# Softmax row sums kept in SBUF two steps at a time, and a re-ordered end of the last image, in a fused attention and involution kernel

## The chip, the cores and the metric

The kernel runs on one core of a Trainium2 chip. A core has a matrix engine (PE, with a separate row PEld for its weight loads), a vector engine (DVE), a scalar engine (ACT), GpSimd (POOL) and a queue engine (SP) that issues most DMAs. Each engine works through its own list of instructions in order; engines wait for one another through semaphores. The on-chip memories are SBUF, and PSUM [...] to which PE writes its results. The metric is the time of one execution on the device in microseconds, as a median of several runs.

## The reference

The input `x` has 4 images of 512 channels and 64x64 pixels, all in float32. Two layers follow each other. The first is self-attention over the 4096 pixels of an image with 128 inner channels, the second an involution (a 7x7 filter whose weights are computed for each pixel and each of 8 groups of 16 channels) between two 1x1 convolutions:

```python
q = jnp.einsum('oc,bcn->bon', wq, xf) + bq[:, None]      # k and v alike
energy = jnp.einsum('bci,bcj->bij', q, k)
attn = jax.nn.softmax(energy, axis=-1)
out = jnp.einsum('bcj,bij->bci', v, attn)
x = jnp.einsum('oc,bcn->bon', wo, out) + bo[:, None] + x

o1 = relu(affine(conv1x1(x, W1), s1, b1))
w = conv1x1(relu(affine(conv1x1(o1, Wr), sr, br)), Ws) + bs      # 49 taps x 8 groups
o2 = sum over the 49 taps of w[tap] * o1 shifted by the tap
return affine(conv1x1(o2, W3), s3, b3) + x
```

## The kernel before

`fast_path` computes the attention without subtracting the row maximum. At its end it checks that every reciprocal of a row sum lies within `SAFE`; the verdict decides at run time whether `general_path`, a slower form, is run after it. With the inputs here it isn't run.

**Stages.** For each image b, `keys_values` (L396) computes keys and values from the 8 chunks of 512 pixels. `attention` (L544) then goes through the chunks of queries. A chunk has 32 steps of 128 keys: PE computes scores into a PSUM tile `pss`, ACT takes their exponential into an SBUF tile `pt` (L562), PE adds `vT`·`pt` to `po` (L586), and DVE adds `pt` to the running sum `pacc` in a PSUM bank (L591 to L596). Scores run two steps ahead. `pt` has five buffers. In the last image the last two chunks are each split into two halves of 256 queries (L548).

**Finishing a chunk.** `finish_block` (L448) is a generator that is advanced between steps of the next chunk. ACT copies `po` to `on`; DVE sums `sums` over 32x32 blocks (L465); PE spreads the row sums with the matmul `pl` (L471); DVE takes the reciprocal, spreads it by a transpose and multiplies `on` (L480). Four matmuls `pwo` and four DVE operations (L487) give the attention output in `xt`, four matmuls `p1` the 1x1 convolution, and transposes `pp` the pixel-major form, which a DMA stores in `pix`. The pauses between these pieces count steps; where `late` is set (L450, the last two chunks of the last image) they wait for the planner's account of times.

**Involution.** A chunk makes two units of four image rows available. `pump` (L213) loads shifted rows of `pix` into `ring`. For a unit, `involution` (L262) has PE compute the filter weights `pw` into two PSUM banks (L250, one buffer), DVE multiply them with `ring` into `prod` tiles (L310, four buffers, 14 to 21 operations), and POOL add these into `acc` (L334) and fold it at the end (L343). `turn_unit` (L349) turns `acc` by PE transposes `pa`, and `close_chunk` (L379) applies the last convolution (`py`, L386) and stores a chunk with one DMA. After the last attention a part of the sums goes to PE (`accp`, L320 to L332); that stretch is the tail.

**The order.** One thread of Python writes all of it out: PE's order is the order of the program with small shifts by the scheduler, and `chores` (L242) advances the three queues of work between attention steps. The account is kept in `pe` (microseconds of PE work issued) and `free` (when DVE, POOL and DMA are expected to be free), fed by `takes`. `pace` (L206) holds the taps to a rate, `until` (L147) waits for a time in the account. Nothing of this is known on the chip[...].

**PSUM.** The eight banks: `s` and `mm` with two buffers each, `w` two banks, `po` one, and `acc` one, which holds `pvt` in the key stage, `pacc` in attention and `accp` in the tail.

Of the kernel before, what the change touches and what calls it, by code (L numbers as in the profile page):

```python
# [14 lines left out]
N = H * W  # L15
P = 128
# [61 lines left out]
def fast_path(  # L78
# [22 lines left out]
    def pool(name, bufs, **kw):  # L101
        return ctx.enter_context(tc.tile_pool(name=name, bufs=bufs, **kw))
# [1 line left out]
    const = pool("const", 1)  # L104
    xpool = pool("x", 6)
    kvpool = pool("kv", 1)
    ptpool = pool("pt", 5)
    redpool = pool("red", 3)
    work1 = pool("work1", 1)
    work2 = pool("work2", 2)  # L110
# [2 lines left out]
    ps = pool("ps", 2, space=bass.MemoryType.PSUM)  # L113
    ps1 = pool("ps1", 1, space=bass.MemoryType.PSUM)

    wt = const.tile([P, O_WR], F32, name="wt")
    vec = const.tile([P, NVEC], F32, name="vec")
    ones = const.tile([P, P], F32, name="ones")
    ident = const.tile([P, P], F32, name="ident")


    rls = const.tile([P, B * N // TB], F32, name="rls")
    quads = const.tile([P, P], F32, name="quads")
    zero = const.tile([WP, PAD, P], F32, name="zero")
    ring = const.tile([P, RING, K, P], F32, name="ring")
# [21 lines left out]
    def until(us):  # L147
        while pe < us and not tail:
            yield "wait"
# [22 lines left out]
    load_x(0, c1)  # L172
    nc.sync.dma_start(wt[:, O_WQ:], wts[:, O_WQ:O_WR])
    nc.gpsimd.memset(ones, 1.0)
    make_identity(nc, ident)
    nc.gpsimd.memset(zero, 0.0)
    for i in range(P // TB):
# [69 lines left out]

    def weights(b, u):
        red, col = reds[b, u]
        pw = ps1.tile([P, NT, CH], F32, tag="w", name=f"pw_{b}_{u}")  # L250
        for t in range(NT):

            rows = slice(t * (P // NT), t * (P // NT) + CR + 1)
            pixels = slice(col + t * P, col + (t + 1) * P)
            mm(
                pw[:, t, : NTAP * G], red[rows, pixels], wt[rows, O_WT : O_WT + NTAP * G],
                shared=2,
            )
        return pw


    def involution():  # L262
        nonlocal low, due
        while True:
# [2 lines left out]
            b, u = units.pop(0)  # L267
            acc = work2.tile([P, NT, 4, P], F32, tag="acc", name=f"acc_{b}_{u}")
            yield from until(free["dve"] + 0.3)
            pw = weights(b, u)  # L270
            begin = pe + 0.5
            accp, ops = None, []
            base = b * STEP + u * UR
# [6 lines left out]
            for o, (x, dy, n) in enumerate(ops):  # L280
                if o and dy >= DYS[1][0] > ops[o - 1][1]:
                    low = base + UR
                    pump()
                rows = [(base + dy + t * 2) % RING for t in range(NT)]
                while base + dy + n + NT > load:
                    yield "wait"
# [51 lines left out]
                yield  # L338
            low = max(low, (b + 1) * STEP if u == NU - 1 else base + UR)
            pump()  # L340
            if accp is None:
                for n in (2, 1):
                    nc.gpsimd.tensor_tensor(  # L343
                        acc[:, :, :n, :], acc[:, :, :n, :], acc[:, :, n : 2 * n, :], ALU.add
                    )
            closing.append(turn_unit(b, u, acc, accp, takes("pool", POOL_OP * 1.5)))


    def turn_unit(b, u, acc, accp, done):  # L349
        c, k = divmod(u, 2)  # L350
        yield from until(done + 2.0)
        for _ in range(7 if tail else 0):
            yield
        last = (b, c) == (B - 1, NCH - 1)
        if last or k == 0:
            sums_c[b, c] = work1.tile([P, CH], F32, tag="accT", name=f"accT_{b}_{c}")
        pa = ps.tile([P, NT, P], F32, tag="mm", name=f"pa_{b}_{u}")
        if accp is None:
            for t in range(NT):
                nc.tensor.transpose(pa[:, t, :], acc[:, t, 0, :], ident)  # L360
            pe_us(0.25)
        else:

            accs = work1.tile([P, CH // P, P], F32, tag="o1t", name=f"accs_{b}_{u}")
            nc.scalar.copy(accs, accp.rearrange("p t d c -> p (t d) c"))
            for t in range(NT):
                parts = [acc[:, t, d, :] for d in range(4)] + [accs[:, 2 * t + d, :] for d in range(2)]
                for i, part in enumerate(parts):
                    mm(pa[:, t, :], part, ident, i == 0, i == len(parts) - 1)
        n = NT * P  # L370
        nc.scalar.copy(sums_c[b, c][:, k * n : (k + 1) * n], pa.rearrange("p t c -> p (t c)"))  # L371
        yield
        if last:
            closing.append(close_chunk(b, c, k * n, n, sums_c.pop((b, c))))
        elif k:
            closing.append(close_chunk(b, c, 0, CH, sums_c.pop((b, c))))


    def close_chunk(b, c, off, n, acc):  # L379
        xt = xs[b, c][:, :, off : off + n]  # L380
        yield
        for t in range(CT):
            py = ps.tile([P, CH], F32, tag="mm", name=f"py_{b}_{c}_{off}_{t}")[:, :n]
            mm(py, w_slice(O_W3, t), acc[:, off : off + n])
            takes("dve", DVE_OP * n / CH)
# [6 lines left out]
        nc.sync.dma_start(out_r[b, :, :, c * CH + off : c * CH + off + n], xt)  # L392


    def keys_values(b):
# [11 lines left out]
        for i, c in enumerate(KEYS):  # L407
# [9 lines left out]
            pk = ps.tile([P, CH], F32, tag="s", name=f"pk_{b}_{c}")  # L417
# [29 lines left out]

    def finish_block(b, c, off, n, po, sums):  # L448

        late = b == B - 1 and c >= NCH - 2  # L450
        name = f"{b}_{c}_{off}"
        xt = xs[b, c][:, :, off : off + n]

        def pause(us, steps):
# [5 lines left out]

        on = work2.tile([P, CH], F32, tag="on", name=f"on_{name}")[:, :n]
        nc.scalar.copy(on, po)
        blocks = work2.tile([P, CH // TB], F32, tag="blocks", name=f"blocks_{name}")
# [5 lines left out]
        pl = ps.tile([P, CH // TB], F32, tag="mm", name=f"pl_{name}")[:, : n // TB]  # L469
        for i in range(CH // n):  # L470
            mm(pl, quads, blocks[:, i * n // TB : (i + 1) * n // TB], i == 0, i == CH // n - 1)  # L471
        row = (b * N + c * CH + off) // TB
        rl = rls[:, row : row + n // TB]
        nc.vector.reciprocal(rl, pl)
        spread = work1.tile([P, CH], F32, tag="rl", name=f"spread_{name}")[:, :n]
        nc.vector.transpose(
            spread.rearrange("p (k q) -> p k q", q=TB),
            rl.unsqueeze(2).broadcast_to([P, n // TB, TB]),
        )
        nc.vector.tensor_tensor(on, on, spread, ALU.mult)  # L480
# [63 lines left out]
    def attention(b, kt, vT):  # L544
        blocks = [(c, 0, CH) for c in range(NCH)]
        if b == B - 1:

            blocks[-2:] = [(c, off, CH // 2) for c in (NCH - 2, NCH - 1) for off in (0, CH // 2)]  # L548

        steps = [(k, j) for k, (_, _, n) in enumerate(blocks) for j in range(N // P * n // CH)]  # L550
        qs, pts, pos, paccs = {}, {}, {}, {}
# [2 lines left out]
        def score(m):  # L554
            k, j = steps[m]
            n = blocks[k][2]
            pss = ps.tile([P, CH], F32, tag="s", name=f"pss_{b}_{k}_{j}")
# [4 lines left out]
            nc.scalar.activation(pt, pss, AF.Exp)  # L562
            pts[m] = pt

        score(0)
        score(1)
        for m, (k, j) in enumerate(steps):
            c, off, n = blocks[k]
            nj = N // P * n // CH
            if j == 0:  # L570
                pos[k] = ps1.tile([P, CH], F32, tag="po", name=f"po_{b}_{k}")[:, :n]
                paccs[k] = ps1.tile([P, CH], F32, tag="acc", name=f"pacc_{b}_{k}")
            if j == 14 and (b, c + 1) not in xs and c + 1 < NCH:
                load_x(b, c + 1)
            if j == 8 and c == NCH - 1 and b + 1 < B:
# [6 lines left out]
            pt = pts.pop(m)  # L582
            for i in range(CH // n):
                key = j * (CH // n) + i
                mm(
                    pos[k], vT[:, key, :], pt[:, i * n : (i + 1) * n],  # L586
                    key == 0, key == N // P - 1,
                )
            takes("dve", DVE_OP)
            if j == 0:  # L590
                nc.vector.tensor_copy(paccs[k], pt)  # L591
            elif j < nj - 1:
                nc.vector.tensor_tensor(paccs[k], paccs[k], pt, ALU.add)  # L593
# [9 lines left out]
    for b in range(B):  # L603
# [23 lines left out]
    nc.tensor.matmul(pn, lhsT=okr, rhs=ones[:, :1], start=True, stop=True)  # L627
    nc.vector.tensor_scalar(verdict, pn, P - 0.5, None, ALU.is_lt)


# [396 lines left out]
```

## Time and profile before

| | |
|---|---|
| Median of 3 runs | 2668.27 us (2666.64 to 2668.32) |
| The profiled execution | 2671.29 us, of which its span 2669.5 us |
| PE busy | 2635.7 us, 99% of the span |
| DVE busy | 1865.3 us, 70%, 2609 instructions |
| POOL busy | 1820.4 us, 68%, 1194 instructions |
| ACT busy | 894.5 us, 34% |
| POOL `acc<-acc,prod` (L334) | 1059 instructions, 1693.0 us, mean 1617 ns |
| DVE `prod<-ring,pw` (L310) | 1092 instructions, 899.9 us |
| DVE `pacc<-pacc,pt` (L593) | 956 instructions, 664.7 us |
| Last `po` of the attention to the end of the span | about 2569 to 2669.5 us |

Busy is the sum of an engine's instruction times, and idle time of an engine that isn't the bound costs nothing. A group's row gives the line, engine and operation, the written and read tiles with their shapes, the count, the busy time, the mean of one, and the idle time ahead of it with what ended it. The engine names with a q (PEq, SPq) are their sequencers.

### The profile page before, as it was taken

What the parts mean: (1) busy time and instruction counts of PE and PEld (TensorE: products, weight loads), DVE (VectorE), ACT (ScalarE), POOL (GpSimd) and SP (SyncE); (2) the same over time, 40 slices, a digit from 0 to 9 for tenths busy, and PEclk for the clock granted to TensorE, in tenths of its full rate; (3) what the DMA queues carried; (4) which work ended last, traced back from release to release, by engine and by line L of the source; (5) the groups of instructions that cost most, each with busy time, mean ns of one, the idle gap of its engine ahead of it and who ended that gap; (6) DMA issues with size and microseconds to landing.
All of it is one profiled execution on the core that took longest, in us unless ns stands there. A gap on an engine that the chain in (4) does not pass through costs nothing.

```text
span 2669.5 us, 22935 instructions
## 1 busy us (share of the span) xinstructions
PE 2635.7 (99%) x6932; PEld 1233.3 (46%) x6932; DVE 1865.3 (70%) x2609; ACT 894.5 (34%) x1495; POOL 1820.4 (68%) x1194
## 2 busy tenths in 40 slices
PE   9999999999999999999999999999999999999997
PEld 4444444444444444444444444444444444446863
DVE  0347788786565777778665778778748477887887
ACT  2333333332333333333233333333323333333320
POOL 0007788788752878878873588778778077887875
PEclk9999999999999999999999999999999999999999
DMA  6032322234604233333441333333461433322532
GB/s 230 0 73 60 91 74 74 63 73 127 158 32 105 59 91 91 91 91 81 126 122 36 73 76 70 91 91 91 107 178 44 101 63 80 78 56 60 104 91 68
DMA packets 104164, 231.60 MB, mean 87 GB/s; under 512 B 5144, under 2 KB 23776, under 8 KB 103904
## 3 DMA queue, kind: packets, MB, share of 16 engines
q1 hardware_dynamic: 103888, 229.96, 34.8%
q8 instruction: 56, 0.92, 0.1%
q14 instruction: 76, 0.62, 0.1%
q10 hardware_dynamic: 144, 0.10, 0.0%
HBM read 187.28 MB, written 42.77 MB: 86 GB/s over the span
## 4 chain that ended last, share of the span: by engine, by line
PE 92%; POOL 3%; DMA 2%; DVE 2%; issue 1%; SPq 0%; ACT 0%; POOLq 0%; DVEq 0%; ACTq 0%
PE pss L194 33%; PE po L194 33%; PE p L194 4%; PE pq L194 4%; PE py L194 4%; PE pwo L194 4%; POOL acc L334 3%; PE pk L194 2%; PE pv L194 2%; PE pw L194 2%; DMA ring<-pix 1%; PE pr L194 1%; DVE prod L310 1%; PE accp L194 1%; PE pp L515 1%
## 5 line engine op out<-in xcount | busy, mean ns | idle before, releaser
L334 POOL TENSOR_TENSOR acc<-acc,prod 128x768 f32<-128x768 f32 (+3 forms) x1059 | 1693.0, 1617 | 823.5 <-DVE prod L310 564.4
L194 PE MATMUL pss<-q,k 128*128 128x512 f32 (+1 forms) x2176 | 1052.4, 570 | 0.0
L194 PE MATMUL po<-pt,v 128*128 128x512 f32 (+1 forms) x2176 | 1047.5, 568 | 0.0
L562 ACT ACTIVATE pt<-pss 128x512 f32<-128x512 f32 x1024 | 611.2, 597 | 1206.0 <-PE pss L194 1168.1
L593 DVE TENSOR_TENSOR pacc<-pacc,pt 128x512 f32<-128x512 f32 x956 | 664.7, 695 | 463.0 <-ACT pt L562 455.7
L310 DVE TENSOR_TENSOR prod<-ring,pw 128x512 f32<-128x512 f32 (+3 forms) x1092 | 899.9, 849 | 107.7 <-POOL acc L334 64.3
L194 PEld LDWEIGHTS po<-pt,v 128*128 128x128 f32 x2176 | 410.9, 190 | 469.8 <-issue 446.1
L194 PEld LDWEIGHTS pss<-q,k 128*128 128x128 f32 x2176 | 403.7, 190 | 448.2 <-issue 435.3
L386 DVE SCALAR_TENSOR_TENSOR x<-py,vec,x 128x512 f32<-128x512 f32 (+1 forms) x132 | 96.3, 731 | 60.7 <-PE py L194 58.6
L194 PE MATMUL pwo<-on,wt 128*128 128x512 f32 (+1 forms) x272 | 132.9, 576 | 3.8 <-DVE on L480 2.7
L194 PE MATMUL py<-accT,wt 128*128 128x512 f32 (+1 forms) x264 | 132.0, 584 | 1.1 <-ACT accT L371 1.0
L194 PE MATMUL p<-x,wt 128*128 128x512 f32 (+1 forms) x272 | 124.6, 584 | 7.3 <-DVE x L487 7.3
L343 POOL TENSOR_TENSOR acc<-acc 128x512 f32<-128x512 f32 x120 | 125.4, 1045 | 9.4
L503 ACT ACTIVATE x<-x,vec 128x512 f32<-128x512 f32 (+1 forms) x136 | 93.8, 694 | 97.9 <-PE p L194 94.2
L194 PE MATMUL pk<-x,wt 128*128 128x512 f32 x256 | 119.0, 605 | 5.1 <-DMA x<-x_dram 5.1
L310 DVE TENSOR_TENSOR acc<-ring,pw 128x1024 f32<-128x1024 f32 (+1 forms) x84 | 78.9, 958 | 60.8 <-PE pw L194 60.3
L194 PE MATMUL pv<-x,wt 128*128 128x512 f32 x256 | 116.8, 593 | 0.0
L194 PE MATMUL pq<-x,wt 128*128 128x512 f32 (+1 forms) x272 | 116.0, 567 | 0.0
L487 DVE SCALAR_TENSOR_TENSOR x<-pwo,bo,x 128x512 f32<-128x512 f32 (+1 forms) x136 | 96.8, 715 | 18.4 <-PE pwo L194 17.2
L194 PEld LDWEIGHTS p<-x,wt 128*128 128x128 f32 x272 | 52.6, 195 | 67.9 <-issue 55.5
L194 PEld LDWEIGHTS pwo<-on,wt 128*128 128x128 f32 x272 | 52.5, 194 | 61.9 <-issue 50.7
L194 PEld LDWEIGHTS pk<-x,wt 128*128 128x128 f32 x256 | 48.8, 194 | 64.8 <-issue 63.6
(58 smaller groups left out, 846.3 us busy)
## 6 DMA issues: line engine op xcount, KB each, us to landing
x<-x_dram SPq DMA_DIRECT2D x55, 1024.0 KB, 5.5
ring<-pix SPq DMA_DIRECT2D x30, 1344.0 KB, 15.2
ring<-pix SPq DMA_DIRECT2D x38, 896.0 KB, 13.4
out_dram<-x SPq DMA_DIRECT2D x31, 1024.0 KB, 4.2
ring<-pix SPq DMA_DIRECT2D x66, 448.0 KB, 10.2
ring<-pix SPq DMA_DIRECT2D x8, 2240.0 KB, 21.3
pix<-o1t SPq DMA_DIRECT2D x60, 128.0 KB, 2.5
ring<-pix SPq DMA_DIRECT2D x8, 224.0 KB, 3.3
```

What stands on the lines that cost most here:

```text
L194: return nc.tensor.matmul(o, lhsT=lhsT, rhs=rhs, start=start, stop=stop)
L310: nc.vector.tensor_tensor(prod[:, :, p0 : p0 + n, :].rearrange("p t d (g c) -> p t d g c", g=G), image.rearrange("p t d (g c) -> p t d g c ...
L334: nc.gpsimd.tensor_tensor(acc[:, :, d0 : d0 + n, :], acc[:, :, d0 : d0 + n, :], prod[:, :, :n, :], ALU.add,)
L343: nc.gpsimd.tensor_tensor(acc[:, :, :n, :], acc[:, :, :n, :], acc[:, :, n : 2 * n, :], ALU.add)
L386: nc.vector.scalar_tensor_tensor(xt[:, t, :], py, v1(V_S3 + t), xt[:, t, :], ALU.mult, ALU.add)
L487: nc.vector.scalar_tensor_tensor(xt[:, t, :], pw, bo[:, t : t + 1], xt[:, t, :], ALU.add, ALU.add)
L503: nc.scalar.activation(xt[:, t, :], xt[:, t, :], AF.Identity, bias=v1(V_B3 + t))
L515: nc.tensor.transpose(pp[:, t, :], o1[:, t * P : (t + 1) * P], ident)
L562: nc.scalar.activation(pt, pss, AF.Exp)
L593: nc.vector.tensor_tensor(paccs[k], paccs[k], pt, ALU.add)
```

## The change

- The running sum `pacc` becomes an SBUF tile of two steps side by side. `pt` tiles hold two steps (three buffers), and DVE adds one pair at a time. The block sum then reads 1024 columns, and `pl` takes twice as many matmuls. `sums` goes.
- The reciprocals are no longer kept for all rows: each block multiplies its two comparisons into a tile `ok` of 16 columns, and the two comparisons over 512 columns at the end go.
- In the last image `late` holds for all chunks, and only the last chunk is split into halves.
- `pss` and `pk` get a PSUM pool of their own, which is closed after the last attention; its two banks hold a second `pw`, so that a unit's weights can be computed while the unit ahead of it is multiplied (`early`).
- In the last image the units from 8 on that are folded before the tail are folded by DVE.
- The half chunks' outputs are stored by four DMAs.

```diff
-    ptpool = pool("pt", 5)
+    ptpool = pool("pt", 3)
...
+    ps_s = scorepool.enter_context(
+        tc.tile_pool(name="ps_s", bufs=2, space=bass.MemoryType.PSUM, reuse_waits="tile")
+    )
+    wpools, early = [ps1], {}
...
-    rls = const.tile([P, B * N // TB], F32, name="rls")
+    ok = const.tile([P, CH // TB], F32, name="ok")
...
     def weights(b, u):
         red, col = reds[b, u]
-        pw = ps1.tile([P, NT, CH], F32, tag="w", name=f"pw_{b}_{u}")
+        wpools.append(wpools.pop(0))
+        pw = wpools[0].tile([P, NT, CH], F32, tag="w", name=f"pw_{b}_{u}")
...
-            pw = weights(b, u)
+            pw = early.pop((b, u), None) or weights(b, u)
...
                     pump()
+                    if tail and units:
+                        early[units[0]] = weights(*units[0])
...
-            if accp is None:
-                for n in (2, 1):
-                    nc.gpsimd.tensor_tensor(
-                        acc[:, :, :n, :], acc[:, :, :n, :], acc[:, :, n : 2 * n, :], ALU.add
-                    )
-            closing.append(turn_unit(b, u, acc, accp, takes("pool", POOL_OP * 1.5)))
+            late = b == B - 1 and u >= NU // 2
+            if accp is None and not late:
+                takes("pool", POOL_OP * 1.5)
+                fold(nc.gpsimd, acc)
+            closing.append(turn_unit(b, u, acc, accp, late, free["pool"]))
...
+        if accp is None and late:
+            yield from until(done + 0.5)
+            done = takes("dve", 1.2)
+            fold(nc.vector, acc)
...
+            if n < CH:
+                nc.sync.dma_start(out_r[b, :, t, c * CH + off : c * CH + off + n], xt[:, t, :])
...
-        late = b == B - 1 and c >= NCH - 2
+        late = b == B - 1
...
-        takes("dve", DVE_OP)
+        takes("dve", 2 * DVE_OP - 0.15)
         nc.vector.tensor_reduce(
-            blocks, sums.rearrange("p (k q) -> p k q", q=TB), AX.X, ALU.add, apply_transpose=True
+            blocks, sums.rearrange("p s (k q) -> p (s k) q", q=TB), AX.X, ALU.add,
+            apply_transpose=True,
         )
...
-        for i in range(CH // n):
-            mm(pl, quads, blocks[:, i * n // TB : (i + 1) * n // TB], i == 0, i == CH // n - 1)
+        groups = 2 * CH // n
+        for i in range(groups):
+            mm(pl, quads, blocks[:, i * nb : (i + 1) * nb], i == 0, i == groups - 1)
...
+        for bound, op in zip(SAFE, (ALU.is_ge, ALU.is_le)):
+            nc.vector.scalar_tensor_tensor(ok[:, :nb], rl, bound, ok[:, :nb], op, ALU.mult)
...
-            blocks[-2:] = [(c, off, CH // 2) for c in (NCH - 2, NCH - 1) for off in (0, CH // 2)]
+            blocks[-1:] = [(NCH - 1, off, CH // 2) for off in (0, CH // 2)]
...
-            pt = ptpool.tile([P, CH], F32, tag="pt", name=f"pt_{b}_{k}_{j}")
-            nc.scalar.activation(pt, pss, AF.Exp)
-            pts[m] = pt
+            if j % 2 == 0:
+                pts[k, j // 2] = ptpool.tile(
+                    [P, 2, CH], F32, tag="pt", name=f"pt_{b}_{k}_{j}"
+                )
+            nc.scalar.activation(pts[k, j // 2][:, j % 2, :], pss, AF.Exp)
...
-                paccs[k] = ps1.tile([P, CH], F32, tag="acc", name=f"pacc_{b}_{k}")
+                paccs[k] = work1.tile([P, 2, CH], F32, tag="pacc", name=f"pacc_{b}_{k}")
...
-            takes("dve", DVE_OP)
-            if j == 0:
-                nc.vector.tensor_copy(paccs[k], pt)
-            elif j < nj - 1:
-                nc.vector.tensor_tensor(paccs[k], paccs[k], pt, ALU.add)
-            else:
-                sums = work1.tile([P, CH], F32, tag="sums", name=f"sums_{b}_{k}")
-                nc.vector.tensor_tensor(sums, paccs.pop(k), pt, ALU.add)
-                f = finish_block(b, c, off, n, pos.pop(k), sums)
+            if j % 2 == 0 and j:
+
+                takes("dve", 2 * DVE_OP - 0.15)
+                first = pts.pop((k, 0)) if j == 2 else paccs[k]
+                nc.vector.tensor_tensor(paccs[k], first, pair, ALU.add)
+            if j == nj - 1:
+                f = finish_block(b, c, off, n, pos.pop(k), paccs.pop(k))
...
     tail.append(True)
+    scorepool.close()
+    wpools.insert(0, pool("ps_w", 1, space=bass.MemoryType.PSUM, reuse_waits="tile"))
+    wpools.reverse()
...
-    ok = const.tile([P, B * N // TB], F32, name="ok")
-    nc.vector.tensor_scalar(ok, rls, SAFE[0], None, ALU.is_ge)
-    nc.vector.scalar_tensor_tensor(ok, rls, SAFE[1], ok, ALU.is_le, ALU.mult)
```

More of the change, by code (lines that the diff above doesn't have):

```diff
@@ L114, in fast_path @@
     ps1 = pool("ps1", 1, space=bass.MemoryType.PSUM)
+    scorepool = ExitStack()
+    ps_s = scorepool.enter_context(
+        tc.tile_pool(name="ps_s", bufs=2, space=bass.MemoryType.PSUM, reuse_waits="tile")
+    )
+    wpools, early = [ps1], {}
     wt = const.tile([P, O_WR], F32, name="wt")
     vec = const.tile([P, NVEC], F32, name="vec")
-    ones = const.tile([P, P], F32, name="ones")
+    ones = const.tile([P, 1], F32, name="ones")
     ident = const.tile([P, P], F32, name="ident")
-    rls = const.tile([P, B * N // TB], F32, name="rls")
+    ok = const.tile([P, CH // TB], F32, name="ok")
     quads = const.tile([P, P], F32, name="quads")
@@ L174, in fast_path @@
     nc.gpsimd.memset(ones, 1.0)
+    nc.gpsimd.memset(ok, 1.0)
     make_identity(nc, ident)
@@ L340, in involution, with fold, turn_unit @@
             pump()
-            if accp is None:
-                for n in (2, 1):
-                    nc.gpsimd.tensor_tensor(
-                        acc[:, :, :n, :], acc[:, :, :n, :], acc[:, :, n : 2 * n, :], ALU.add
-                    )
-            closing.append(turn_unit(b, u, acc, accp, takes("pool", POOL_OP * 1.5)))
-    def turn_unit(b, u, acc, accp, done):
+            late = b == B - 1 and u >= NU // 2
[3 more added lines that the diff above has]
+            closing.append(turn_unit(b, u, acc, accp, late, free["pool"]))
+    def fold(engine, acc):
+        for n in (2, 1):
+            engine.tensor_tensor(
+                acc[:, :, :n, :], acc[:, :, :n, :], acc[:, :, n : 2 * n, :], ALU.add
+            )
+    def turn_unit(b, u, acc, accp, late, done):
         c, k = divmod(u, 2)
+        if accp is None and late:
+            yield from until(done + 0.5)
+            done = takes("dve", 1.2)
+            fold(nc.vector, acc)
         yield from until(done + 2.0)
@@ L391, in close_chunk @@
         takes("dma", X_US)
-        nc.sync.dma_start(out_r[b, :, :, c * CH + off : c * CH + off + n], xt)
+        if n == CH:
+            nc.sync.dma_start(out_r[b, :, :, c * CH + off : c * CH + off + n], xt)
     def keys_values(b):
@@ L416, in keys_values @@
             xt = xs[b, c] if c < KEEP else xs.pop((b, c))
-            pk = ps.tile([P, CH], F32, tag="s", name=f"pk_{b}_{c}")
+            pk = ps_s.tile([P, CH], F32, tag="s", name=f"pk_{b}_{c}")
             for t in range(CT):
@@ L462, in finish_block @@
         nc.scalar.copy(on, po)
-        blocks = work2.tile([P, CH // TB], F32, tag="blocks", name=f"blocks_{name}")
-        takes("dve", DVE_OP)
+        blocks = work2.tile([P, 2 * CH // TB], F32, tag="blocks", name=f"blocks_{name}")
+        takes("dve", 2 * DVE_OP - 0.15)
         nc.vector.tensor_reduce(
-            blocks, sums.rearrange("p (k q) -> p k q", q=TB), AX.X, ALU.add, apply_transpose=True
+            blocks, sums.rearrange("p s (k q) -> p (s k) q", q=TB), AX.X, ALU.add,
+            apply_transpose=True,
         )
         yield from pause(free["dve"], 3)
-        pl = ps.tile([P, CH // TB], F32, tag="mm", name=f"pl_{name}")[:, : n // TB]
-        for i in range(CH // n):
-            mm(pl, quads, blocks[:, i * n // TB : (i + 1) * n // TB], i == 0, i == CH // n - 1)
-        row = (b * N + c * CH + off) // TB
-        rl = rls[:, row : row + n // TB]
+        nb = n // TB
+        pl = ps.tile([P, CH // TB], F32, tag="mm", name=f"pl_{name}")[:, :nb]
+        groups = 2 * CH // n
+        for i in range(groups):
+            mm(pl, quads, blocks[:, i * nb : (i + 1) * nb], i == 0, i == groups - 1)
+        rl = work2.tile([P, CH // TB], F32, tag="rlb", name=f"rl_{name}")[:, :nb]
         nc.vector.reciprocal(rl, pl)
@@ L477, in finish_block @@
             spread.rearrange("p (k q) -> p k q", q=TB),
-            rl.unsqueeze(2).broadcast_to([P, n // TB, TB]),
+            rl.unsqueeze(2).broadcast_to([P, nb, TB]),
         )
         nc.vector.tensor_tensor(on, on, spread, ALU.mult)
+        for bound, op in zip(SAFE, (ALU.is_ge, ALU.is_le)):
+            nc.vector.scalar_tensor_tensor(ok[:, :nb], rl, bound, ok[:, :nb], op, ALU.mult)
         takes("dve", 0.3 + DVE_OP * n / CH)
@@ L556, in score @@
             n = blocks[k][2]
-            pss = ps.tile([P, CH], F32, tag="s", name=f"pss_{b}_{k}_{j}")
+            pss = ps_s.tile([P, CH], F32, tag="s", name=f"pss_{b}_{k}_{j}")
             for i in range(CH // n):
@@ L560, in score @@
                 mm(pss[:, i * n : (i + 1) * n], kt[:, key : key + P], qs[k])
-            pt = ptpool.tile([P, CH], F32, tag="pt", name=f"pt_{b}_{k}_{j}")
-            nc.scalar.activation(pt, pss, AF.Exp)
-            pts[m] = pt
+            if j % 2 == 0:
+                pts[k, j // 2] = ptpool.tile(
+                    [P, 2, CH], F32, tag="pt", name=f"pt_{b}_{k}_{j}"
+                )
+            nc.scalar.activation(pts[k, j // 2][:, j % 2, :], pss, AF.Exp)
         score(0)
@@ L581, in attention @@
                 score(m + 2)
-            pt = pts.pop(m)
+            pair = pts[k, j // 2]
+            pt = pair[:, j % 2, :]
             for i in range(CH // n):
@@ L626, in fast_path @@
     pn = ps.tile([1, 1], F32, tag="mm", name="pn")
-    nc.tensor.matmul(pn, lhsT=okr, rhs=ones[:, :1], start=True, stop=True)
+    nc.tensor.matmul(pn, lhsT=okr, rhs=ones, start=True, stop=True)
     nc.vector.tensor_scalar(verdict, pn, P - 0.5, None, ALU.is_lt)
```

## The prediction

> **What bounds the kernel now.** I read the chain of waits first, then the groups by shape, then busy time by stage, then single instructions in order of time. The chain and three groups:
>
> ```profile
> PE 92%; POOL 3%; DMA 2%; DVE 2%; issue 1%; SPq 0%; ACT 0%; POOLq 0%; DVEq 0%; ACTq 0%
> ...
> L593 DVE TENSOR_TENSOR pacc<-pacc,pt 128x512 f32<-128x512 f32 x956 | 664.7, 695 | 463.0 <-ACT pt L562 455.7 <-DVE pacc L593 0.5
> ...
> L310 DVE TENSOR_TENSOR prod<-ring,pw 128x1024 f32<-128x1024 f32 x264 | 312.5, 1211 | 1.4 <-POOL acc L334 1.4
> ...
> L480 DVE TENSOR_TENSOR on<-on,spread 128x512 f32<-128x512 f32 x30 | 33.8, 1126 | 0.7
> ```
>
> The matrix engine (PE) sets the time; its stream is ordered at build time, so a late partner costs only where PE reaches an instruction that needs it. The groups' last numbers are what to see: a 512-wide sum with one operand in PSUM takes 695 ns and a 1024-wide product 1211, while `on<-on,spread`, 512 wide with both operands in SBUF, averages 1126. The busy times of four chunks of image 1 (columns: window, its length, then PE, PEld, DVE, ACT, POOL):
>
> ```profile
> 844.40:913.70 69.30, 69.30 (x170) 30.67 (x169) 54.72 (x75) 25.58 (x43) 53.16 (x32) 1.00 0.28 59
> 913.70:988.10 74.40, 74.40 (x185) 32.57 (x183) 57.21 (x81) 27.08 (x45) 56.80 (x38) 1.00 0.34 82
> 988.10:1060.80 72.70, 72.70 (x182) 32.22 (x181) 57.11 (x87) 25.92 (x43) 59.35 (x44) 1.00 0.34 83
> 1060.80:1131.40 70.60, 70.60 (x176) 31.34 (x176) 55.87 (x78) 24.75 (x41) 59.62 (x36) 1.00 0.35 86
> ```
>
> Over the six chunks 2 to 7 of image 1, a chunk is 72.3 us long and POOL is busy 57.5 of it, so it has some 15 us to spare, in gaps of 2 to 7 us. Why `on` is slow, from the time order (start, length, engine):
>
> ```profile
> 204.58 4.79 POOL L334 TENSOR_TENSOR acc<-acc,prod 128x1024 f32<-128x1024 f32 x2 [200.98 <-DVE prod L310]
> ...
> 208.02 1.89 DVE L480 TENSOR_TENSOR on<-on,spread 128x512 f32<-128x512 f32 x1
> ...
> 347.02 0.69 DVE L480 TENSOR_TENSOR on<-on,spread 128x512 f32<-128x512 f32 x1
> 347.24 2.41 POOL L343 TENSOR_TENSOR acc<-acc 128x512 f32<-128x512 f32 x2
> ...
> 1024.03 2.08 POOL L343 TENSOR_TENSOR acc<-acc 128x512 f32<-128x512 f32 x2
> ```
>
> At 208.02 `on` meets a POOL sum in flight (one ends near 209.37) and ends at 209.91: 0.69 us of work after that sum. At 347 it comes first, takes 0.69, and POOL's two folds last 2.41 us; undisturbed they last 2.08. So the two exclude each other, both ways.
>
> [...] the product row has 1211, so I take 1.22.
>
> **The change part by part.**
>
> *Sums of exponentials.* Per chunk of 32 steps, 32 DVE operations (one copy, 31 sums, 0.695 us, 22.2 us) become 15 of 1024 elements (18.3 us alone): 479 in all, 31 chunks of 15 and two half chunks of 7. In DVE work alone this gains 3.9 us a chunk, worth nothing, since DVE waits for ACT (455.7 us before `pacc`). But the sum moves from PSUM to SBUF[...]. 75 fall where POOL has nothing (chunks 0 and 1 of image 0, chunk 1 of images 1 to 3: 7.5 us of POOL in 69 there). For the other 404:
> - DVE waits for the POOL sum in flight. POOL's groups (255 of 2.36, 297 of 1.82, 427 of about 1.29, 200 of 0.73 us) give a mean remainder of sum(t²)/(2·sum(t)) = 0.88 us; `on` shows 0.43 on average, as many of its turns fall in gaps. About 12 us a chunk: DVE goes from 57 to 57-22.2+18.3+12 plus 1.5 for smaller edits = 67 of 72 us. Tight, not yet the bound.
> - POOL is held. A 0.69 us `on` cost the folds 0.34 (and 0.52 at 565.6), some 0.26 less than its length, so 1.22 costs 0.95; full length is the other end. Per chunk 14.3 to 18.3 us; with POOL's 57.5 that is 71.8 to 75.8 of 72.3 us. [...] the spare time is used up.
>
> What reaches PE: a sum comes every 4.8 us, so in a stretch without gap POOL falls behind 0.2 us per us. In image 1 POOL runs from 1053.0 to 1098.5 with no real gap: 3 us late at the fold ending 1068.6, whose transpose `pa` on PE comes 2.8 us later (1071.46); another 6 at the next, where PE's `pw` at 1097.52 waits for the DVE products that ended at 1091.2 (6.3 us margin, less DVE's own lateness, as four product buffers tie it to POOL). The gaps after that (2.5 and 6.6 us) take the rest. With `pl` and `pwo`, which follow DVE by 2.5 to 5 us, I take 3.5 us of PE stall a chunk: 24 such chunks (2 to 7, four images) = 84, and 3 each for chunk 0 of images 1 to 3 = 9. Bounds: 0 (gaps swallow all) to 9 (no gap refilled and 1.22 lost each). [...]
>
> *The `pt` buffers.* Five of one step become three of two: a slot comes up again five steps (8.6 us) after its exp in both, in the changed kernel three (5.2 us) for a chunk's first pair. No cost on its own; it passes a DVE lateness over 4 to 7 us on to ACT and PE.
>
> *Row sums.* The transposing reduce goes from 512 to 1024 [...], and `pl` needs twice the matmuls. PE starts in time order show a single `pl` adds 0.23 us to the stream and two add 0.45: 30 chunks x 0.22, two half chunks x 0.44, and chunk 6 saves 0.45 as one instead of two halves: +7 us on PE, not hidden. Bounds 5 to 10.
>
> *Verdict.* Two 16-column operations a chunk on DVE (some 0.2 us each) beside other work. In the tail L622 (0.93) and L623 (1.75, in the chain) go: -2.6.
>
> *Last image.* `late` now holds for all eight chunks: `pl`, `pwo` and `pp` are placed 0.8 us after the planner's time for DVE. That planner prices a double sum at 1.25 [...], so PE comes too early: 6 chunks x 2 = +12 (0 to 30). In exchange unit 12's weights now stand 12 rows (10 us) ahead of the last `po`; before, they come 6.4 us behind it. POOL and DVE are still shared there, so half: -8. Chunk 6 is no longer halved: equal columns on PE, nothing.
>
> *Second banks.* The tail idles 1.26, 1.76 and 1.66 us on DVE waiting for `pw` (2599.9, 2618.2, 2637.7): -4.5. Last output by quarters: SP issues each behind its own sum: -1. The four late units folded on DVE cost it 4 x 1.1 us plus waits, with POOL relieved: 0.
>
> Sum: 93+7-2.6+12-8-4.5-1 = +96. Span 2669.5+96 = 2765; the profiled run was 2671.29 (1.8 outside the span), 3.0 above the median of 2668.27, so 2764: I say 2765.
>
> **The rivals.**
> - *Gaps swallow it (not slower).* One mechanism: POOL's 14.8 us of spare time per chunk. It decides if a sum costs POOL 0.95 us or less and lateness stays under 2.8 us at `pa`. Then +7-16 = 2659. For it: 71.8 is under 72.3, PE has margins everywhere, and the double sums thin out DVE. Against: the spare time lies in few gaps, while lateness is made evenly.
> - [...] Each sum costs 1.22+0.88 on DVE and 1.22 on POOL, the pair blocks in turn: 27 chunks at +8 or more = 216, with the other terms about 2890. For it: DVE at 67 of 72 in strict order, with evacuations, sums and products in one queue. Against: PE stalls hold back the sums, and POOL catches up in them and in the next image's key stage (64.5 of 78.7 us busy).
> - [...] (some property of the 1024 shape): same end as the first. Against: the final L623, also two SBUF operands, took 1.75 beside a POOL fold.
>
> **How the numbers follow.** Forecast 0.66, [...] not slower 0.11 (0.09 the first, 0.02 the third). The forecast's own range is 2700 to 2840; adding [...] part of the second rival, 2685 to 2885 holds 8 in 10. Within 0.2% (5 us, what this measurement can tell from nothing) is 0.02, faster 0.09, slower 0.89.
>
> **What would show it.** `pacc` in the changed profile: about 1.9 us mean instead of 1.22 (right)[...]. POOL's L344 sums longer by some 10 to 20% for the same shapes. PE idle or stretched before `pa` and `pw` behind POOL and DVE, chunks 2 to 7 near 76 us, chunk 1 unchanged. `pl` at 0.45 us. A tail about 16 us shorter. I am wrong if chunks 2 to 7 keep 72 us with `pacc` at 1.9: then the margins were larger than I read.

## The result, and the profile after

The changed kernel took 2830.77 us (median of 5 runs, 2823.91 to 2831.33), the kernel before 2668.32 us in the same session. The ratio is 1.06, with a 95% interval of 1.0586 to 1.0615: slower by 6%, or 162 us. The forecast was 2765 us, the range 2685 to 2885.

From the page of the changed kernel, the chain of waits by engine and by line:

```profile
PE 51%; POOL 17%; DVE 16%; issue 8%; DMA 6%; ACT 0%; SPq 0%; POOLq 0%; DVEq 0%; ACTq 0%
PE pss L201 17%; PE po L201 17%; POOL acc L344 16%; DVE pacc L623 5%; DVE prod L320 5%; DMA ring<-pix 5%; PE p L201 3%; PE pq L201 3%; PE py L201 2%; PE pv L201 2%; PE pwo L201 2%; DVE ok L507 2%; PE pk L201 1%; PE accp L201 1%; PE pw L201 1%
```

PE had 92% of the chain before. Now POOL's sums and DVE have a third of it: in that third these engines, not the matrix engine, decide when the next step begins. The groups by shape show what became slow:

```profile
L623 DVE TENSOR_TENSOR pacc<-pacc,pt 128x1024 f32<-128x1024 f32 x446 | 780.7, 1750 | 271.7 <-ACT pt L592 268.8 <-DVE pacc L623 0.5
L344 POOL TENSOR_TENSOR acc<-acc,prod 128x1024 f32<-128x1024 f32 x258 | 715.9, 2775 | 464.1 <-DVE prod L320 388.0 <-PE pq L201 48.2 <-PE pss L201 10.5
L344 POOL TENSOR_TENSOR acc<-acc,prod 128x768 f32<-128x768 f32 x297 | 643.2, 2166 | 80.2 <-DVE prod L320 58.8
L507 DVE SCALAR_TENSOR_TENSOR ok<-rl,ok 128x16 f32<-128x16 f32 x62 | 64.3, 1037 | 0.0
L505 DVE TENSOR_TENSOR on<-on,spread 128x512 f32<-128x512 f32 x31 | 32.5, 1048 | 0.0
```

and POOL's sums in the kernel before:

```profile
L334 POOL TENSOR_TENSOR acc<-acc,prod 128x1024 f32<-128x1024 f32 x255 | 602.7, 2364 | 544.1 <-DVE prod L310 311.8 <-PE po L194 211.7 <-PE pa L194 3.0
L334 POOL TENSOR_TENSOR acc<-acc,prod 128x768 f32<-128x768 f32 x297 | 540.0, 1818 | 105.2 <-DVE prod L310 83.6
```

The double sum takes 1750 ns on average. POOL's 1024-wide sums take 2775 where they took 2364 before, its 768-wide ones 2166 where they took 1818, for the same data: the time for which POOL is held shows as a longer record (the second experiment below takes this apart). And `ok`, on 16 columns, takes 1037 ns.

In the time order of one chunk, both sides of the exclusion are plain (start, length, engine):

```profile
1058.81 10.35 POOL L344 TENSOR_TENSOR acc<-acc,prod 128x256 f32<-128x256 f32 x9
...
1064.30 2.35 DVE L623 TENSOR_TENSOR pacc<-pacc,pt 128x1024 f32<-128x1024 f32 x1
...
1069.21 1.22 DVE L623 TENSOR_TENSOR pacc<-pacc,pt 128x1024 f32<-128x1024 f32 x1 [1.56 <-ACT pt L592]
1069.23 3.14 POOL L360 TENSOR_TENSOR acc<-acc 128x512 f32<-128x512 f32 x2
```

At 1064.30 POOL is in the middle of a run of sums and the double sum takes 2.35 us. At 1069.21 it comes first and takes 1.22, and the two folds of POOL, which start 0.02 us later, take 3.14 us in place of 2.08. The whole trace says the same: 99 of the 479 double sums start while none of POOL's operations on `acc` is in flight, and none of these 99 takes over 1.25 us; of the other 380, 303 take longer, 2.05 us on average. The busy times of the four chunks in image 1 that answer to those shown before (window, length, then PE, PEld, DVE, ACT, POOL):

```profile
875.70:950.30 74.60, 70.59 (x169) 30.78 (x168) 61.63 (x56) 25.60 (x43) 64.07 (x30) 0.98 0.26 54
950.30:1024.00 73.70, 73.25 (x183) 32.23 (x182) 64.05 (x66) 25.97 (x43) 69.60 (x39) 1.00 0.34 82
1024.00:1102.50 78.50, 73.78 (x183) 32.22 (x182) 65.43 (x72) 25.99 (x44) 72.15 (x44) 1.00 0.32 77
1102.50:1180.50 78.00, 73.82 (x183) 32.07 (x182) 68.88 (x64) 26.13 (x44) 73.50 (x36) 1.00 0.32 78
```

POOL was busy 57 of 72 us; now it is busy or held for 64 to 73 of 74 to 78 us, and PE has up to 4.7 us without work. Where PE waits is seen in the chain of the third of these chunks, in order of time:

```profile
1027.30 1.63 DVE pacc L623
1029.13 0.71 DVE spread L501
1029.84 0.79 DVE ok L507
1030.63 1.13 DVE acc L320
1031.76 1.28 DVE on L505
1033.04 1.16 DVE ok L507
1034.20 2.26 DVE prod L320 x2
1036.46 2.46 DVE pacc L623
...
1041.23 3.30 POOL acc L344
1044.61 2.36 POOL acc L344
1047.04 3.21 POOL acc L344
1050.34 2.37 POOL acc L344
1053.06 2.05 DVE pacc L623
1055.83 1.12 PE pwo L201 x2
```

The start of a chunk is where DVE has most to do: the last chunk's row sums, the first products of a unit, and the new sums stand in one queue. Five of these eight DVE lines have two operands in SBUF. The products then wait for POOL (3.30 and 3.21 us where a sum had 2.36), and the last of the four `pwo` pairs starts at 1055.83, 31.8 us after the last copy of `po` of the chunk ahead (1024.01); before the change it stood 26.2 us after it. Over the whole execution the longest waits of PE are these (total, times, longest):

```profile
PE pwo L201 <- DVE x L514: 26.8, 21, 1.8
PE pl L201 <- DVE blocks L488: 24.7, 11, 4.8
PE pwo L201 <- DVE on L505: 19.1, 6, 6.5
PE py L201 <- DVE x L514: 17.8, 11, 2.1
PE py L201 <- DVE x L406: 15.4, 4, 8.4
PE pa L380 <- POOL acc L360: 14.9, 11, 3.3
```

Here a wait cost more than its length. After PE has waited 2.94 us for a block sum, the next pairs of matmuls start up to 1.70 us apart in place of 0.86:

```profile
805.34 0.62 PE L201 MATMUL pl<-blocks,quads 128*128 128x16 f32 x4 [2.94 <-DVE blocks L488]
805.81 1.10 PE L201 MATMUL pss<-q,k 128*128 128x512 f32 x2
806.75 1.66 PE L201 MATMUL po<-pt,v 128*128 128x512 f32 x2
808.21 1.91 PE L201 MATMUL pss<-q,k 128*128 128x512 f32 x2
809.91 1.27 PE L201 MATMUL po<-pt,v 128*128 128x512 f32 x2
811.02 1.02 PE L201 MATMUL pss<-q,k 128*128 128x512 f32 x2
811.88 1.02 PE L201 MATMUL po<-pt,v 128*128 128x512 f32 x2
```

The trace holds the clock that PE was granted: from 807.0 on it was at half for 3.4 us. The changed kernel has 13 such stretches, 82 us in all, of which 11 begin during an idle stretch of PE of 2.0 us or more, or within 2 us after it; PE has 21 idle stretches of that length, and 10 of them had no such stretch behind them. The kernel before has five, 30 us in all. The mean granted clock is 0.986 against 0.995; from it, an estimate: 26 us of the 152 by which the span grew are lost to the clock (82 against 30 us at half).

### The profile page after: what moved, and what is told of

It reads as the page before. It is cut to its first block, busy times and chain, and to the rows that moved or that the text cites. A ratio compares the mean times of both kernels' runs of the same rounds, so it can differ in the third digit from the quotient of the medians.

```text
span 2821.9 us, 21227 instructions
## 1 busy us (share of the span) xinstructions
PE 2672.5 (95%) x6830; PEld 1211.5 (43%) x6830; DVE 2093.7 (74%) x2128; ACT 894.6 (32%) x1486; POOL 2172.7 (77%) x1190
## 4 chain that ended last, share of the span: by engine, by line
PE 51%; POOL 17%; DVE 16%; issue 8%; DMA 6%; ACT 0%; SPq 0%; POOLq 0%; DVEq 0%; ACTq 0%
PE pss L201 17%; PE po L201 17%; POOL acc L344 16%; DVE pacc L623 5%; DVE prod L320 5%; DMA ring<-pix 5%; PE p L201 3%; PE pq L201 3%; PE py L201 2%; PE pv L201 2%; PE pwo L201 2%; DVE ok L507 2%; PE pk L201 1%; PE accp L201 1%; PE pw L201 1%
## 5 line engine op out<-in xcount | busy, mean ns | idle before, releaser
L344 POOL TENSOR_TENSOR acc<-acc,prod 128x768 f32<-128x768 f32 (+3 forms) x1062 | 2034.3, 1933 | 626.4 <-DVE prod L320 526.9
L623 DVE TENSOR_TENSOR pacc<-pacc,pt 128x1024 f32<-128x1024 f32 x446 | 780.7, 1750 | 271.7 <-ACT pt L592 268.8
L201 PEld LDWEIGHTS po<-pt,v 128*128 128x128 f32 x2112 | 401.6, 191 | 486.1 <-issue 466.3
L201 PEld LDWEIGHTS pss<-q,k 128*128 128x128 f32 x2112 | 394.2, 192 | 459.7 <-issue 443.1
L201 PE MATMUL pwo<-on,wt 128*128 128x512 f32 (+1 forms) x264 | 137.4, 614 | 46.9 <-DVE x L514 26.8
L360 POOL TENSOR_TENSOR acc<-acc 128x512 f32<-128x512 f32 x112 | 136.6, 1219 | 8.8
L201 PEld LDWEIGHTS py<-accT,wt 128*128 128x128 f32 x264 | 48.7, 192 | 99.4 <-issue 39.7
## 6 DMA issues: line engine op xcount, KB each, us to landing
ring<-pix SPq DMA_DIRECT2D x30, 896.0 KB, 13.7
```

Source lines behind the costliest of these rows:

```text
L201: return nc.tensor.matmul(o, lhsT=lhsT, rhs=rhs, start=start, stop=stop)
L344: nc.gpsimd.tensor_tensor(acc[:, :, d0 : d0 + n, :], acc[:, :, d0 : d0 + n, :], prod[:, :, :n, :], ALU.add,)
L360: engine.tensor_tensor(acc[:, :, :n, :], acc[:, :, :n, :], acc[:, :, n : 2 * n, :], ALU.add)
L623: nc.vector.tensor_tensor(paccs[k], first, pair, ALU.add)
```

## The experiments

Each was run beside the kernel before, which had a median of 2668.4 to 2668.8 us over all its runs.

**Pair sums alone.** Edit on the kernel before:

```diff
-                paccs[k] = ps1.tile([P, CH], F32, tag="acc", name=f"pacc_{b}_{k}")
+                paccs[k] = work1.tile([P, 2, CH], F32, tag="pacc", name=f"pacc_{b}_{k}")
...
+            if j % 2 == 0 and j:
+                takes("dve", 2 * DVE_OP - 0.15)
+                first = pts.pop((k, 0)) if j == 2 else paccs[k]
+                nc.vector.tensor_tensor(paccs[k], first, pair, ALU.add)
```

with `pt` in pairs, the block sum over 1024 columns and the doubled `pl`.

> The kernel before with one part of the change alone: the sums of exponentials by pairs in SBUF, with the block sum over 1024 columns and the doubled pl that belong to them. [...] (pair sums and POOL's sums exclude each other): pacc at a mean of 1.7 to 1.8 us, POOL's 1024-wide sums at 2.7 us instead of 2.36, chunks 2 to 7 at 75 to 77 us, in all 2745 to 2785 us. Rival (the other edits, the verdict's 62 operations and the last image's order above all, made the loss): pacc may be as slow, but the time stays under 2700 us.

Measured: 2786.52 us, ratio 1.0447 (1.0429 to 1.0464). By shape:

```profile
L599 DVE TENSOR_TENSOR pacc<-pacc,pt 128x1024 f32<-128x1024 f32 x444 | 825.6, 1859 | 255.2 <-ACT pt L569 252.1
L334 POOL TENSOR_TENSOR acc<-acc,prod 128x1024 f32<-128x1024 f32 x256 | 707.9, 2765 | 460.6 <-DVE prod L310 437.6 <-PE pss L194 3.5 <-PE pa L194 3.0
```

118 of the 162 us come with this one part (the sum is 0.06 us and the time 1.5 us above the upper end of what was expected). POOL's busy time rises from 1820.4 to 2171.5 us, by 351: 0.87 us for each of the 404 sums that can meet POOL at work. Chunks 2 to 7 of image 1 take 74.5 us on average, just under the 75 to 77 expected.

**The same sum with one operand in PSUM.** The changed kernel, where the double sum adds a constant from a PSUM bank. It leaves out the row sums and adds a `memset` per chunk:

```diff
+                other = ps1.tile([P, CH], F32, tag="acc", name=f"other_{b}_{k}")
+                nc.vector.memset(other, 0.5)
...
-                nc.vector.tensor_tensor(paccs[k], first, pair, ALU.add)
+                nc.vector.tensor_tensor(
+                    paccs[k], pair, other.unsqueeze(1).broadcast_to([P, 2, CH]), ALU.add
+                )
```

> The changed kernel, where the pair sum adds to the pair a constant tile of one PSUM bank, read twice, in place of the running sum: as many DVE operations of the same length with the same waits for ACT and the same pt buffers, but with one SBUF operand only (a memset per chunk is added; the row sums are left out). [...] the operation takes 1.2 us with little spread, POOL's sums fall back, time 2670 to 2715 us. Rival (it is the grain: an operation of 1.2 us every second step, fewer pt slots, a later block sum): time stays over 2780 us, with 1.2 us operations.

Measured: 2680.6 us, ratio 1.0048 (1.0031 to 1.0065). By shape:

```profile
L344 POOL TENSOR_TENSOR acc<-acc,prod 128x1024 f32<-128x1024 f32 x258 | 609.6, 2363 | 536.1 <-DVE prod L320 468.7 <-PE pq L201 49.6 <-PE pss L201 1.3
L625 DVE TENSOR_TENSOR pacc<-pt,other 128x1024 f32<-128x1024 f32 x479 | 582.5, 1216 | 458.9 <-ACT pt L592 457.3
```

The shape, count, place in the order and `pt` buffers are those of the changed kernel; what differs is where one operand lies, and that a sum no longer reads the sum ahead of it. The sum takes 1216 ns, POOL's takes 2363 as before the change, and 150 us are gone. Of its 479 sums 339 start beside a POOL operation in flight, and none takes over 1.25 us. That a sum reads the one ahead of it isn't the cause: in the changed kernel such sums took 1.2 us too wherever POOL was not in flight. So neither the length of the operation, nor the fewer `pt` buffers, nor the longer block sum made the loss, but the second operand in SBUF beside a working POOL: with it a sum took 1750 ns and POOL's 1024-wide sum 2775, without it 1216 and 2363.

**Everything but the pair sums.** The changed kernel with single sums in a PSUM bank, as before:

```diff
-                paccs[k] = work1.tile([P, 2, CH], F32, tag="pacc", name=f"pacc_{b}_{k}")
+                paccs[k] = ps1.tile([P, CH], F32, tag="acc", name=f"pacc_{b}_{k}")
```

and what belongs to it (five `pt` buffers, block sum over 512 columns, one `pl`).

> The changed kernel with that part alone undone: sums step by step in a PSUM bank, five buffers of pt, block sum over 512 columns, single pl. Verdict, last image and second banks stay as changed. [...] POOL's sums back near their undisturbed 2.36 us at 1024 but for the waits that on and ok cause, time 2665 to 2700 us: the verdict costs some 10 to 20, the last image's order some 10, the tail gives 8 back. Rival (the other edits made the loss): over 2740 us.

Measured: 2672.43 us, ratio 1.0016 (1.0009 to 1.0023). PE has 86% of the chain again. By itself the rest of the change costs 3.7 us; most of the 44 us that it costs on top of the pair sums are there only beside them. Against this kernel the one with the constant from PSUM is 8.2 us slower. That is about the 7 us that the prediction gave the doubled `pl`, which that experiment keeps; it was not measured apart.

**The verdict from PSUM.** In the changed kernel:

```diff
-        for bound, op in zip(SAFE, (ALU.is_ge, ALU.is_le)):
-            nc.vector.scalar_tensor_tensor(ok[:, :nb], rl, bound, ok[:, :nb], op, ALU.mult)
+        for bound, op in zip(SAFE, (ALU.is_le, ALU.is_ge)):
+            nc.vector.scalar_tensor_tensor(ok[:, :nb], pl, 1 / bound, ok[:, :nb], op, ALU.mult)
```

> The changed kernel, where the verdict's two operations a block read the sums pl from PSUM with the reciprocal bounds instead of rl from SBUF, so that only one operand lies in SBUF. [...] from a mean of 1.04 us to 0.2 us, 50 us less DVE time of which about half stood in the chain: 2795 to 2815 us. Rival (they wait beside other waits, so nothing is gained): 2825 to 2835 us.

Measured: 2805.98 us, ratio 1.0517 (1.05 to 1.0535), 24.8 us less than the changed kernel.

```profile
L507 DVE SCALAR_TENSOR_TENSOR ok<-pl,ok 128x16 f32<-128x16 f32 x62 | 7.5, 122 | 0.0
```

The operation itself is worth 122 ns; the other 915 of its 1037 went when its operand came from PSUM, and so count as the wait for POOL. The place of the operand costs nothing of its own: the shortest `ok` of the changed kernel, with both operands in SBUF, took 124 ns. Some 57 us of DVE time go, and a good 40% of them stood on the path. In the version with single sums, where DVE has room, the same edit brought 6.4 us (below).

**Finishing by the account of times.** The changed kernel with

```diff
-        late = b == B - 1
+        late = b == B - 1 and c >= NCH - 2
```

The question is whether an account without DVE's waits for POOL places PE's instructions too early.

> The changed kernel with late back to the last two chunks of the last image; everything else as changed. [...] the last image's attention, 569 us in the changed kernel against 539 where only the pair sums were changed, gets 20 to 30 us shorter, the tail some us longer, in all 2800 to 2815 us. Rival (the last image is longer because of its folds on DVE, and units begun earlier): 2825 to 2835 us.

Measured: 2820.66 us, ratio 1.0565 (1.0548 to 1.0581), 10 us less: the miss is the tail. The attention of the last image, from its first to its last copy of `po`, fell from 569.3 to 546.5 us as expected, but the tail grew from 90.6 to 103.2 us. So the account loses 23 us in the attention and gives 13 back at the end. These are single executions: up to the first of these copies, where the two kernels are alike, they took 2162.0 and 2173.9 us, so a few us between kernels with pair sums are for the medians to tell.

**Both small undos together.** The two edits above in one kernel.

> The changed kernel with both small undos: the verdict from PSUM (alone: 24.8 us less) and late for the last two chunks only (alone: 10 us less). If the two losses are separate, 2790 to 2800 us, near the 2786.5 of the pair sums alone; if they are one wait seen twice, 2803 to 2810.

Measured: 2804.71 us, ratio 1.051 (1.0494 to 1.0526): no better than the verdict alone, as expected if the two losses are one wait. But the stages don't show one wait. Beside the verdict from PSUM the account's undo still shortens the attention of the last image, from 559.3 to 544.6 us; the tail takes that back, 103.9 in place of 85.9. At the start of that tail DVE waits in order for POOL's last sum before a fold, and the last pair sum, the block sum and PE's `pl` stand behind it:

```profile
2708.58 1.15 DVE L360 TENSOR_TENSOR acc<-acc 128x512 f32<-128x512 f32 x2 [5.45 <-POOL acc L344]
2709.65 1.22 DVE L623 TENSOR_TENSOR pacc<-pacc,pt 128x1024 f32<-128x1024 f32 x1
2710.90 1.25 DVE L488 TRANSPOSE_TENSOR_REDUCE blocks<-pacc 128x32 f32<-128x1024 f32 x1
...
2712.20 1.88 PE L201 MATMUL pl<-blocks,quads 128*128 128x8 f32 x8 [11.70 <-DVE blocks L488]
```

The kernel with the account's undo alone has the same wait of 11.7 us, the one with the verdict alone none over 4.8. 18 us remain between this and the pair sums alone. The mean granted clock of PE is 0.984 here and 0.991 there, which is an estimated 20 us, as much as remains: longer single waits, up to 4.3 us at `pwo` and 11.7 at `pl`, against 5.2 at most there, go with the lower mean clock. In the last image DVE waits 19.2 us for POOL's last sum before its folds:

```profile
DVE acc L360 <- POOL acc L344: 19.2, 4, 5.6
```

How much of the 18 us that makes was not tried with pair sums in place.

**Towards a faster version.** Six kernels with single sums in a PSUM bank followed. The first takes the version without pair sums above and adds the edit that reads the verdict from PSUM; the rest is as changed:

> The changed kernel with the sums step by step in PSUM again and the verdict read from PSUM; last image and second banks as changed. Against the same with the verdict from SBUF (2672.4 us): if the verdict's waits stand on the path there too, 2662 to 2668 us; if the spare time of DVE hides them once the pair sums are gone, 2670 to 2673.

2666.01 us, ratio 0.9992 (0.9985 to 0.9998). The verdict's waits did stand on the path. The second adds the edit that sets `late` for the last two chunks only:

> The same as the version with sums and verdict from PSUM, with late back to the last two chunks of the last image. Theory: the last image's attention loses the 12 us that it gained there (516.9 against 504.5 us), the tail keeps some of its gain of 10 us: 2655 to 2665 us, faster than both kernels. Rival (the account's early finish is what shortens the tail): no gain, 2665 to 2672.

2670.45 us, ratio 1.0008 (1.0001 to 1.0015). The rival was right: attention 508.7 in place of 514.2 us, but tail 95.0 in place of 85.6. What costs 10 us with pair sums earns 4 without. The third is the kernel before with the second banks alone:

```diff
-        pw = ps1.tile([P, NT, CH], F32, tag="w", name=f"pw_{b}_{u}")
+        wpools.append(wpools.pop(0))
+        pw = wpools[0].tile([P, NT, CH], F32, tag="w", name=f"pw_{b}_{u}")
...
+                    if tail and units:
+                        early[units[0]] = weights(*units[0])
```

> The kernel before with the second pair of weight banks alone. By the sum of the prediction 4.5 us of waits for pw in the tail go: 2662 to 2666 us. Rival (DVE is full in the tail, so the weights' wait is only exchanged for another): 2667 to 2670.

2665.62 us, ratio 0.9987 (0.9981 to 0.9994): a gain of 2.8 us where 4.5 had been forecast. The fourth is the first of these with the four folds back on POOL:

```diff
-            late = b == B - 1 and u >= NU // 2
+            late = False
```

> The version with sums and verdict from PSUM (2666.0 us), with the four late units of the last image folded by POOL as before in place of DVE. There the DVE folds wait 13.6 us in all for POOL's last sum, with sums and products queued behind them. If that wait reaches PE: 2658 to 2663 us; if the queue has room: 2664 to 2668.

2657.7 us, ratio 0.9959 (0.9945 to 0.9972). The folds on DVE thus cost 8.3 us: in the version with them they took 4.5 us of work and 13.6 us of waiting for POOL's last sum, with everything behind them in DVE's queue held:

```profile
DVE acc L360 <- POOL acc L344: 13.6, 4, 5.0
```

The last two start from there and split two chunks again, without and with the account for the whole last image. Without it, this is the kernel before with the second banks, the verdict from PSUM and the outputs by quarters:

```diff
-            blocks[-1:] = [(NCH - 1, off, CH // 2) for off in (0, CH // 2)]
+            blocks[-2:] = [(c, off, CH // 2) for c in (NCH - 2, NCH - 1) for off in (0, CH // 2)]
```

> The kernel before with the second banks (2665.6 us alone), the verdict on 16 columns read from PSUM, and the half chunks' outputs stored by quarters: all of the change that touches no attention step. By the prediction's sum 2.6 and 1.0 us more: 2660 to 2664 us, faster than both kernels. Rival (these operations stood beside other waits): 2665 to 2668.

> As f2, with the account of times (late) for all chunks of the last image. The attention of the last image gains some 10 us of time, the tail loses them (with DVE folds it was 514.2 and 85.6 against 508.7 and 95.0 us). Theory (without the pair sums the account fits the chip, so its early units pay): 2656 to 2662 us. Rival: 2662 to 2668.

2660.17 us, ratio 0.9966 (0.9952 to 0.9979), and 2656.47 us, ratio 0.9954 (0.994 to 0.9968). Both beat both kernels, by 0.3 and 0.5% against the kernel before. The second has the lowest median, though its runs (2655.27 to 2657.86) overlap those of the fourth version (2656.42 to 2659.56): single sums in PSUM, verdict on 16 columns read from PSUM, the account for the last image, second weight banks, folds on POOL, outputs by quarters, two chunks split. Its attention in the last image is 510.8 us and its tail 78.3, against 504.5 and 98.3 in the kernel before.

## Why the prediction was right, and where its sum was short

- *The mechanism.* Right: DVE and POOL exclude each other, both ways, at the sums that meet POOL at work. The experiment with the operand from PSUM shows it apart from everything else: 1216 ns in place of 1750 for DVE's sum, 2363 in place of 2775 for POOL's at 1024.
- *Wait of DVE for POOL.* Forecast 0.88 us a sum, 1.9 us in all. Measured 1.75, which is (479 x (1.748-1.216))/404 = 0.63 us for each that can meet POOL: between the 0.43 that `on` showed and the remainder of a random arrival. The 303 sums that did wait lost 0.84 us each, so the price of a wait was right and the number of waits too high.
- *Hold of POOL by a sum.* Forecast 0.95 us from the two folds; measured 0.87.
- *What reaches PE.* Forecast 93 us of stall and 7 of `pl`. Pair sums alone made the span 112.8 us longer (2782.3 against 2669.5). By the copies of `po`, the 24 chunks 2 to 7 grew by 88.6 us (84 of stall and some 5 of `pl` forecast), the keys and first chunks of images 1 to 3 by 11.9 (9 forecast) and chunk 1 of these images by 14.9 (nothing forecast), while the tail shrank by 2.9. In size this step held. It is partly luck, since it has no term for the granted clock (0.991 against 0.995, an estimated 12 us of the 112.8). And 3.5 us a chunk was picked between bounds of 0 and 9, with margins worked out for `pa` and `pw`, while PE of the changed kernel waits mostly elsewhere: 46.9 us at `pwo`, 33.7 at `py` and 24.7 at `pl`, nearly all of it behind DVE, against 16.5 at `pa` and 2.6 at `pw`. Nor did chunk 1 stay unchanged: it takes 76.8 us in place of 71.6, and 71.9 with the operand from PSUM. One reading was off by a little: the 72.3 us a chunk were taken over 844.4 to 1278.2, some 5 us past the last copy. From copy to copy it is 71.2 us with POOL busy for 56.7, so the spare time of 15 us stands; in the changed kernel these chunks take 75.3.
- *Verdict.* The step that failed most: "Two 16-column operations a chunk on DVE (some 0.2 us each) beside other work". `rl` and `ok` both lie in SBUF, and they waited for POOL as well: 1.04 us each against 0.12 with `pl` from PSUM, and 24.8 us on the path. The term was -2.6 and should have been some +22 beside pair sums (with single sums the edit brought 6.4). What `on` had shown (1.89 us beside a POOL sum, 0.69 alone) was applied to the pair sums and not to these lines of the diff; size was taken for the price where the wait is the price.
- *Last image.* "+12 (0 to 30)" for the account and "-8" for the earlier unit: measured 23 and -13, net 10 where 4 was forecast. Right in kind; with the verdict's waits gone it is 15 and -18, and nothing is left to gain by undoing it. Chunk 6 in halves or whole, equal columns: in the trace before, PE's score and `po` matmuls start 216 ns apart at 256 columns and 429 at 512 (medians).
- *Second banks and output.* Forecast -4.5, measured -2.8 for the banks alone. The tail as a whole went from 98.3 to 90.6 us, by 8 where 16 had been added up.
- *Folds on DVE.* Forecast 0; they cost 8.3 us with single sums. They need POOL's last sum, and held DVE's queue for 13.6 us in all until it was there. With pair sums no run takes their price apart; their share in the 11.7 us wait at `pl` is seen in a trace only.

The shortfall of 66 us is thus in the edits that were priced at little: 118 of the loss belong to the pair sums, for which 100 were forecast, and 44 to the rest on top of them, for which -4 were. By itself the rest costs 3.7, so a sum of separate terms missed that these edits meet the pair sums in the same queue and wait for the same engine. The lower clock, an estimated 26 us in all, is in no term. The rival at 2890, which had been given 0.23, was too high; the forecast's reason, that PE's stalls let POOL catch up, fits POOL busy or held for 77% of the span, but wasn't tested.

## What to carry to other kernels

Before a sum is moved from PSUM to SBUF, count the DVE instructions that then have two SBUF operands while POOL works, and price each with a wait for POOL and a hold of POOL; halving the number of operations and a shorter sum are no gain if each waits 0.6 us for POOL and holds it 0.9, as here. Small operations counted like long ones here (`ok` waited 0.9 us on 16 columns), and reading one operand from PSUM took 24.8 us off. And where the order is written from an account of times, an engine's wait that the account doesn't know is paid by whoever stands behind it; the same edit can then gain in one version and lose in the next.

## What the runs showed of the hardware

A DVE operation on 16 columns with both operands in SBUF took 1037 ns on average beside a busy POOL (124 ns at its shortest), and 122 ns with one of them in PSUM. No 1024-wide sum with both operands in SBUF took over 1.25 us when no POOL operation was in flight at its start; 303 of the 380 others did. A held POOL instruction showed no idle time here: its record got longer (2775 against 2363 ns at 128x1024), POOL's busy share rose from 68% to 77% for the same data, and a busier engine was the sign of a blocked one. And the changed kernel's trace has PE's clock at half in 13 stretches of 3.4 to 13.7 us; 11 of them began at idle stretches of PE of 2.0 us or more, of which there were 21 (mean clock 0.986, before the change 0.995).
